# Seven products for the first 512 context rows of a Perceiver layer, one between any two heads, and a head's turn on VectorE one head later

## The chip, the core and the metric

The kernel runs on one core of a Trainium2 chip. The metric is the device time of one execution in microseconds (us), as a median over runs. TensorE multiplies, VectorE (DVE in the profile), ScalarE (ACT) and GpSimd (POOL) work on elements, and SyncE (SP) issues most transfers (DMA). Each engine works through its own queue in order and waits on semaphores for the others. TensorE writes to PSUM banks of 128 x 512 float32, which VectorE and ScalarE empty. All data are float32.

## The reference, cut to what matters

A layer of a Perceiver: 256 tokens of width 512 attend to themselves (causally) and to 4096 context rows; a state-space block and a mixture of experts follow. Only the attention's beginning is touched.

```python
xn = layernorm(x)                                    # 256 x 512
q  = rope(rms_norm((xn @ wq) by 16 heads of 128))
k  = rope(rms_norm((xn @ wk) by 4 heads)),  v = xn @ wv
k_ctx = rms_norm((ctx @ wk_ctx) by 4 heads)          # ctx: 4096 x 512
v_ctx = ctx @ wv_ctx
out = softmax([q k_ctx^T, q k^T + causal] / sqrt(128)) @ [v_ctx, v]
```

## The kernel before

The context is cut into eight chunks of 512 rows (`CK`). For chunk c, `kT` holds the keys turned, `v` the values and `r` the keys' factors. Attention runs in nine stages: stage 0 over the tokens' own keys, stage s over chunk s-1. While a stage's scores and values run on TensorE, the next chunk's keys and values are made between them.

Chunks 1 to 7 (`fast_steps`) use a scheme of seven products instead of eight: the chunk's rows and its inner dimension form a 2x2 block matrix (a11 to a22), and the weights form another, b11 and b21 being the two halves of wk_ctx and b12 and b22 those of wv_ctx. Keys are a11 b11 + a12 b21 and so on. Sums of the blocks, S1 to S4 on the left and T1 to T4 on the right, are multiplied, and the products are added up into keys and values. Each of the seven is split in seven again. T1, T2 and T4 come from `weight_sums` on POOL (L338 to L340) and T3 from one VectorE sum in place in `last_sum` (L389).

Chunk 0, made before stage 0, does not use the scheme. `context_pieces(0)` gives four key pieces, four value pieces and four transposes, one of each for every 128 rows; a piece is a projection of four matmuls 128x128 by 128x512 (`project`, L225), emptied by ScalarE (L319 for keys, L325 for values).

The tokens' projections come as "heads": `k_of(t)` and `q_of(j, t)` for two row tiles t and four groups j. A head (`self_block`) is one projection of four matmuls into a bank of `ps_mm` (two banks), then `norm_rope`: ScalarE copies the bank to `raw` (L536) and squares it (L262); VectorE does four rope steps (L541 to L544) and scales the square sums (L199); POOL takes the power -1/2 (L200) and multiplies (L545). Then the result is turned so that the head dimension is on partitions: for all but the last group by `turn_heads`, which is a VectorE block transpose (L268) and five DMAs on SP (L271, L273), else by TensorE transposes (`selfT`, L575).

The order is written out by hand in one tuple of steps, value and key pieces between the heads:

```python
for f in (ctx_v[0], lambda: k_of(0), lambda: k_of(1), last_key, *q[0], ctx_v[1], weights_of, lambda: self_value(0),
          q[1][0], one, q[1][1], one, lambda: self_value(1), weights_of, q[2][0], one, q[2][1], one, ctx_v[2],
          q[3][0], two, q[3][1], two, ctx_v[3]):
```

Ahead of the tuple stand the layernorm of both tiles, the key pieces 0 to 2, the transposes of xn into xT (`turn_xn`: L216 on TensorE, L220 on VectorE) and the rope tables (L528, L529). `one`, `two` and `weights_of` prepare the second level's weights on POOL and ScalarE. The framework's planner puts each engine's instructions in a queue largely in this order, moving one ahead where another must wait; `tc.issue_after(ins)` puts what is traced under it behind `ins` on the same engine. PSUM pools in this path: `ps_tp` one bank, `ps_mm` two, `ps_sc` three (scores), `ps_oT` two. A branch on the size of the norm weights picks this path (`bounded`); the other is not run here.

Loads are issued by SP in program order: pieces of ctx chunk 0 and of wk_ctx, x, the rest of ctx, wv_ctx, wk, wq0, wv, wq1 to wq3, and the context chunks 1 and 2.

Of the kernel before, what the change touches and what calls it, by code (L numbers as in the profile page):

```python
# [75 lines left out]
def perceiver_layer(ctx: ExitStack, tc: tile.TileContext, a: dict, out: bass.AP):  # L76
# [64 lines left out]
    def layer(ctx, bounded):  # L141
# [71 lines left out]
        def turn_xn(t, tp, halves=False):  # L213

            for k in range(KD):
                TE.transpose(tp[:, k * P:(k + 1) * P], xn[:, t, k * P:(k + 1) * P], ident)  # L216

            for copy, ks in (((V.tensor_copy, slice(0, KD // 2)), (S.copy, slice(KD // 2, KD))) if halves else
                             ((V.tensor_copy, slice(0, KD)),)):
                copy(xT[:, ks, t * P:(t + 1) * P], tp.rearrange("p (k n) -> p k n", k=KD)[:, ks])  # L220

        def project(ps, lhs, rhs_of):

            for k in range(KD):
                TE.matmul(ps, lhs(k), rhs_of(k), start=(k == 0), stop=(k == KD - 1))  # L225
# [14 lines left out]
        qT = qp.tile([P, NT, NH, P], FP, tag="qT", name="qT")  # L240
        aT = qT

        ctx_tiles = {0: ctx0}
# [12 lines left out]
        def head_squares(raw, apart=False):  # L256
# [53 lines left out]
        def context_pieces(c):  # L310

            ct = ctx_tiles.pop(c)
            v, r, raws, key_transpose, _ = context_tiles(c)

            def key_piece(i):
                ps = ps_mm.tile([P, 512], FP, tag="mm", name="ps_k")
                project(ps, lambda k: ct[:, i, k, :], lambda k: wkc[:, k, :])
                raws[i] = raw = krp.tile([P, NKV, HD], FP, tag="kraw" if i == 1 else "kn", name="kraw")
                S.copy(raw, ps.rearrange("p (h d) -> p h d", d=HD))  # L319
                key_rms(raw, r[:, i, :])  # L320

            def value_piece(i):
                ps = ps_mm.tile([P, 512], FP, tag="mm", name="ps_v")
                project(ps, lambda k: ct[:, i, k, :], lambda k: wvc[:, k, :])
                S.copy(v[:, i, :], ps)  # L325

            return [[lambda i=i, f=f: f(i) for i in range(CK // P)] for f in (key_piece, value_piece, key_transpose)]

        fast = {}

# [50 lines left out]

        each = lambda steps: [None for _ in steps]

        def last_sum():

            V.tensor_tensor(b12, b22, b12, ALU.subtract)  # L389
            each(second_sums("wv"))  # L390

        three = ring([(ps_mm, "mm"), (ps_mm, "mm"), (ps_tp, "tp")] if bounded else [(ps_mm, "mm")])

        def fast_steps(c, behind=None):
# [136 lines left out]
        heads_done = []  # L531

        def norm_rope(ps, t, tb):

            raw = krp.tile([P, REP, HD], FP, tag="kraw", name="raw")
            S.copy(raw, ps)  # L536
            r = small.tile([P, REP], FP, tag="r", name="r")
            power_half(r, head_squares(raw), 1.0 / HD, 1e-6, REP)
            cs, sn = (tb[:, i, t, :].unsqueeze(1).to_broadcast([P, REP, HD]) for i in range(2))
            o, u = take_ro(), take_ru()  # L540
            V.tensor_tensor(o, raw, cs, ALU.mult)  # L541
            V.tensor_tensor(u[:, :, 0:HALF], raw[:, :, HALF:HD], sn[:, :, 0:HALF], ALU.mult)
            V.tensor_tensor(u[:, :, HALF:HD], raw[:, :, 0:HALF], sn[:, :, HALF:HD], ALU.mult)
            V.tensor_tensor(o, o, u, ALU.add)  # L544
# [7 lines left out]
        ctx_k, ctx_v, ctx_t = context_pieces(0)  # L552
        for t in range(NT):
            normed = layernorm(t)
        for i in range(3):
            ctx_k[i]()
        for t in range(NT):
            turn_xn(t, ps_sc.tile([P, 512], FP, tag="sc", name="lnT"))
        rope_table(tab_k, kw_bc)
        rope_table(tab_q, qw_bc)  # L560
        with tc.issue_after(normed.ins):
            weight_sums(*sums)

        def self_block(t, w, tb, dst):
            ps = ps_mm.tile([P, 512], FP, tag="mm", name="ps_self")
            project(ps, lambda k: xT[:, k, t * P:(t + 1) * P], lambda k: w[:, k, :])
            o = norm_rope(ps.rearrange("p (h d) -> p h d", d=HD), t, tb)

            if bounded and w is not wq[3]:
                return turn_heads(dst, o, qd.pop())  # L570

            def turn():
                tp = ps_tp.tile([P, REP, P], FP, tag="tp", name="selfT")
                for h in range(REP):
                    TE.transpose(tp[:, h, :], o[:, h, :], ident)  # L575
                S.copy(dst, tp)
            return turn
# [10 lines left out]
        turns = ctx_t[0:3]  # L588

        def last_key():  # L590
            ctx_k[3]()
            return ctx_t[3]

        placed = fast_weights(sums)
        early = {"t": second_sums("t"), "t4": second_sums("t4")}
# [1 line left out]
        def behind_head(group, n=1):  # L597
            with tc.issue_after(heads_done[-1]):
                for _ in range(n):
                    next(early[group])  # L600

        weights_of = lambda: next(placed)
        one, two = lambda: behind_head("t"), lambda: behind_head("t4", 2)
        for f in (ctx_v[0], lambda: k_of(0), lambda: k_of(1), last_key, *q[0], ctx_v[1], weights_of, lambda: self_value(0),
                  q[1][0], one, q[1][1], one, lambda: self_value(1), weights_of, q[2][0], one, q[2][1], one, ctx_v[2],
                  q[3][0], two, q[3][1], two, ctx_v[3]):
            turn = f()
            if f not in (weights_of, one, two):
                turns.append(turn)
            while len(turns) > 2:  # L610
                turn = turns.pop(0)
                if turn:
                    turn()
# [17 lines left out]

        pin = tc.keep_in_program_order
        pin(nc.sync.dma_start(by_channel, a["by_channel"]))
        pin(nc.sync.dma_start(by_head, a["by_head"].partition_broadcast(P)))


        next(placed)
# [14 lines left out]
        def bounded_attention(beside):  # L652

            pp = pool("pp", 4)
            bq = small.tile([P, 3], FP, tag="bq", name="bq", bufs=1)
            V.tensor_reduce(bq[:, 0:1], qw_bc, AX.X, ALU.max, apply_absolute_value=True)
            V.tensor_reduce(bq[:, 1:2], kw_bc, AX.X, ALU.max, apply_absolute_value=True)
# [50 lines left out]
            for s in range(NC + 1):  # L708
# [39 lines left out]
        def general_attention():  # L748
            with ExitStack() as gctx:
# [11 lines left out]
                stats = {}  # L761
                for turn in turns:
                    turn()
                last_sum()
# [1050 lines left out]
```

## Time and profile before

| | |
|---|---|
| median of 3 runs | 960.36 us (959.47 to 961.25) |
| profiled execution | 961.0 us |
| its span on the core | 959.2 us |
| granted TensorE clock | 0.998 |
| TensorE busy | 939.9 us (98%) |
| VectorE, ScalarE, POOL busy | 571.4, 383.0, 429.3 us |
| data moved | 124.93 MB |

The span runs from the first to the last instruction that the profile holds; 1.8 us of the execution lie around it. In rows of the profile, "x8" counts records. A float32 matmul leaves two records, a float32 transpose one. "L225" is a line of the kernel, here that of the helper that records all projections, so tiles' names (ps_k, ps_v, ps_self) tell them apart. The arrow in square brackets names what ended an idle time.

| stretch, us | TensorE busy | VectorE | ScalarE | POOL |
|---|---|---|---|---|
| 0 to 5.4 | 0.00 | 0.70 | 0.00 | 1.33 |
| 5.4 to 18 | 12.55 | 6.06 | 5.66 | 2.27 |
| 18 to 24 | 6.00 | 3.80 | 3.17 | 5.84 |
| 24 to 30 | 6.00 | 2.13 | 3.09 | 4.17 |
| 30 to 40 | 10.00 | 5.51 | 8.42 | 4.58 |
| 40 to 50 | 10.00 | 3.64 | 3.95 | 4.09 |
| 50 to 60 | 10.00 | 6.13 | 5.82 | 3.91 |
| 60 to 70 | 10.00 | 7.17 | 4.97 | 6.73 |
| 70 to 80 | 10.00 | 6.93 | 5.28 | 7.64 |
| 80 to 90 | 10.00 | 7.62 | 7.57 | 9.82 |
| 90 to 100 | 9.89 | 9.62 | 6.10 | 9.95 |

The heads and pieces take until about 79 us; stage 0 follows, and stage 1 begins at about 101 us.

### The profile page before, as it was taken

What the parts mean: (1) busy time and instruction counts of PE and PEld (TensorE: products, weight loads), DVE (VectorE), ACT (ScalarE), POOL (GpSimd) and SP (SyncE); (2) the same over time, 40 slices, a digit from 0 to 9 for tenths busy, and PEclk for the clock granted to TensorE, in tenths of its full rate; (3) what the DMA queues carried; (4) which work ended last, traced back from release to release, by engine and by line L of the source; (5) the groups of instructions that cost most, each with busy time, mean ns of one, the idle gap of its engine ahead of it and who ended that gap; (6) DMA issues with size and microseconds to landing.
All of it is one profiled execution on the core that took longest, in us unless ns stands there. A gap on an engine that the chain in (4) does not pass through costs nothing.

```text
span 959.2 us, 10117 instructions
## 1 busy us (share of the span) xinstructions
PE 939.9 (98%) x3025; PEld 508.0 (53%) x3025; DVE 571.4 (60%) x1205; ACT 383.0 (40%) x872; POOL 429.3 (45%) x487
## 2 busy tenths in 40 slices
PE   7999999999999999999999999999999999999996
PEld 3444555555555555555555555544465655555442
DVE  4458766566566656665756656658497666632223
ACT  3646444344344444343443444443253742122221
POOL 3559956345444644634724723300013234545542
PEclk9999999999999999999999999999999999999999
DMA  9732053053034015104205203360046453899983
GB/s 328 241 78 47 0 176 87 1 154 89 1 86 141 15 35 174 35 14 152 77 1 153 67 1 88 81 228 0 0 157 209 165 196 122 327 328 366 362 322 109
DMA packets 130803, 124.93 MB, mean 130 GB/s; under 512 B 80017, under 2 KB 99250, under 8 KB 125490
## 3 DMA queue, kind: packets, MB, share of 16 engines
q1 hardware_dynamic: 119216, 77.96, 26.9%
q0 software_dynamic: 7904, 40.90, 11.7%
q10 hardware_dynamic: 3618, 5.33, 1.5%
q8 instruction: 26, 0.43, 0.2%
q14 instruction: 39, 0.32, 0.1%
HBM read 88.76 MB, written 35.41 MB: 129 GB/s over the span
## 4 chain that ended last, share of the span: by engine, by line
PE 95%; issue 1%; POOL 1%; DVE 1%; DMA 1%; ACT 0%; SPq 0%; POOLq 0%; DVEq 0%
PE oT L693 24%; PE scT L668 24%; PE ps_kv L459 15%; PE ps_egu L225 5%; PE ps_self L225 4%; PE ps_v L225 2%; PE ps_o L892 2%; PE ps_xbc L225 2%; PE ps_k L225 2%; PE ps_ye L1616 2%; PE ps_out L1089 1%; PE ps_z L225 1%; PE ps_sgu L225 1%; PE ps_ye L1619 1%; PE xgTp L1495 1%
## 5 line engine op out<-in xcount | busy, mean ns | idle before, releaser
L684 DVE TENSOR_TENSOR lacc<-lacc,prT 128x512 f32<-128x512 f32 x256 | 200.6, 785 | 197.3 <-ACT prT L674 196.2
L674 ACT ACTIVATE prT<-scT,bq,rk 128x512 f32<-128x512 f32 x256 | 198.4, 775 | 280.4 <-PE scT L668 269.5
L668 PE MATMUL scT<-qT,kT 128*128 128x512 f32 x536 | 273.5, 592 | 0.0
L693 PE MATMUL oT<-prT,v 128*128 128x512 f32 x528 | 269.4, 592 | 0.1
L693 PEld LDWEIGHTS oT<-prT,v 128*128 128x128 f32 x528 | 100.1, 190 | 125.8 <-issue 117.9
L668 PEld LDWEIGHTS scT<-qT,kT 128*128 128x128 f32 x536 | 101.2, 190 | 41.0 <-issue 30.6
L459 PE MATMUL ps_kv<-fast,ctx 128*128 128x256 f32 x350 | 99.6, 379 | 0.0
L459 PEld LDWEIGHTS ps_kv<-fast,ctx 128*128 128x128 f32 x350 | 66.4, 190 | 48.3 <-issue 39.9
L410 POOL TENSOR_TENSOR ctx<-ctx 128x128 f32<-128x128 f32 x21 | 11.4, 542 | 98.7 <-PE ps_kv L459 98.7
L200 POOL TENSOR_TENSOR rk<-pv,mhalf 128x4 f32<-128x4 f32 x32 | 37.4, 1180 | 28.0 <-DVE pv L199 28.0
L262 ACT ACTIVATE xn<-kraw 128x128 f32<-128x128 f32 x112 | 33.5, 301 | 39.4 <-POOL kraw L434 22.1
L459 PE MATMUL ps_kv<-wkv,ctx 128*128 128x256 f32 x168 | 48.9, 379 | 0.0
L444 POOL TENSOR_TENSOR v<-fast,v 128x768 f32<-128x768 f32 x21 | 40.9, 1960 | 16.2 <-DVE fast L488 15.6
L459 PEld LDWEIGHTS ps_kv<-wkv,ctx 128*128 128x128 f32 x168 | 31.8, 190 | 28.4 <-issue 25.0
L699 DVE TENSOR_TENSOR oacc<-oT,oacc 128x512 f32<-128x512 f32 x64 | 43.6, 682 | 0.0
L1599 DVE TENSOR_TENSOR hid<-si,ps_egu 128x128 f32<-128x128 f32 x18 | 5.2, 287 | 47.5 <-ACT si L1597 47.5
L459 PE MATMUL ps_kv<-fast,fast 128*128 128x256 f32 x112 | 33.3, 379 | 0.0
L459 PEld LDWEIGHTS ps_kv<-fast,fast 128*128 128x128 f32 x112 | 21.3, 190 | 17.8 <-issue 12.0
L268 DVE STREAM_TRANSPOSE tr<-kraw 128x512 f32<-128x512 f32 x28 | 18.3, 690 | 19.6 <-POOL kraw L433 19.6
L892 PE MATMUL ps_o<-wo,qT 128*128 128x512 f32 x64 | 28.8, 592 | 0.0
L1290 POOL DMA_INDIRECT xg_sb<-xg,place x16 | 15.1, 947 | 29.1 <-PE xgTp L1495 26.7
L225 PE MATMUL ps_self<-wq,xT 128*128 128x512 f32 x64 | 28.1, 592 | 0.0
(439 smaller groups left out, 1412.8 us busy)
## 6 DMA issues: line engine op xcount, KB each, us to landing
xg<-xn SPq DMA_DIRECT2D x6, 2560.0 KB, 9.4
ctx<-in_ctxT_dram SPq DMA_DIRECT2D x7, 1024.0 KB, 5.0
kd<-tr SPq DMA_DIRECT2D x112, 64.0 KB, 2.2
kT<-kd SPq DMA_DIRECT2D x28, 256.0 KB, 3.0
ye<-y_sb ACTq DMA_DIRECT2D x19, 256.0 KB, 8.3
wq<-in_wq_dram SPq DMA_DIRECT2D x4, 1024.0 KB, 14.4
wo<-in_wo_dram SPq DMA_DIRECT2D x4, 1024.0 KB, 7.9
w_in<-in_W_inT_dram SPq DMA_DIRECT2D x4, 1024.0 KB, 8.7
```

The costliest lines, as they stand in the source:

```text
L200: return G.tensor_tensor(dst, v[:, :n], mhalf[:, :n], ALU.pow)
L225: TE.matmul(ps, lhs(k), rhs_of(k), start=(k == 0), stop=(k == KD - 1))
L262: S.activation(sq[:, h, :], raw[:, h, :], AF.Square, accum_out=ss[:, h:h + 1])
L444: G.tensor_tensor(to[:, 1:4], q, base[:, 1:4], ALU.add)
L459: TE.matmul(b[n], sets[name][i], y, start=start, stop=True, skip_group_check=True)
L668: scored.append(TE.matmul(sc, kT[:, g, i * P:(i + 1) * P], qT[:, t, heads4(g), :].rearrange("p h q -> p (h q)"), start=True, stop=True).ins)
L674: S.activation(pr, sc, AF.Exp, bias=shift, scale=SCALE if r is None else r[:, i, g:g + 1])
L684: V.tensor_tensor(la, la, pr, ALU.add)
L693: TE.matmul(outs[g, t], v[:, i, g * HD:(g + 1) * HD], pr, start=(n == 0), stop=last)
L699: V.tensor_tensor(ov, outs.pop((g, t)), ov, ALU.add)
L892: TE.matmul(m["ps_o", t], aT[:, t, h, :], wo[j][:, h % 4, :], start=(h == 0), stop=(h == NH - 1))
L1616: TE.matmul(ps[i], h[:, i, :], wd[i], start=True, stop=False)
```

## The change

Chunk 0 is made by the seven products as well, one level deep: each product is two row blocks (j = 0, 1) of two matmuls 512 wide. p1 and p2 run before xn is turned: p1(j) = a11 b11 is copied by ScalarE to v, then p2(j) = a12 b21 is added into the same bank, and the sum is copied as the first keys. The others stand one between any two heads. They are emptied by VectorE, which adds each to what v holds. The sums S1 to S4 are made by VectorE in a tile that borrows a buffer of the context chunks, T3's sum moves up behind the second head, and the remaining POOL sums of wv_ctx move into the first sums of chunk 1. The loads change their order: x ahead of the second half of wk_ctx, the second half of ctx chunk 0 and wk (in two halves) ahead of wv_ctx, chunk 2 behind the small tables of a later block. A head's turn by VectorE is kept back until the next head's operations have been issued, and several small VectorE operations are put behind the copies of xT. The keys' transposes write to `ps_sc` instead of `ps_tp`.

```diff
     load_ctx0(0, 1)
     load_wkc(0, 1)
     load_wkc(1, 1)
-    load_wkc(2, 2)
+    load_ctx0(1, 1)
     nc.sync.dma_start(x_sb, a["x"].rearrange("(t p) d -> p t d", p=P))
-    load_ctx0(1, 1)
-    load_ctx0(2, 2)
-    nc.sync.dma_start(wvc, a["wv_ctx"].rearrange("(k p) n -> p k n", p=P))
+    load_wkc(2, 1)
+    load_wkc(3, 1)
...
         def load_ctx(c):
             ct = ctxp.tile([P, CK // P, KD, P], FP, tag="ctx", name="ctx")
-            nc.sync.dma_start(ct, a["ctxT"][c])
+            with tc.issue_after(settled[0]) if c == 2 else nullcontext():
+                nc.sync.dma_start(ct, a["ctxT"][c])
...
-        wk = wpiece(a["wk"], "wk")
+        load_ctx0(2, 2)
+        wk = wpool.tile([P, KD, 512], FP, tag="w", name="wk")
+        for k in (0, 2):
+            nc.sync.dma_start(wk[:, k:k + 2, :], a["wk"][k * P:(k + 2) * P, :].rearrange("(k p) n -> p k n", p=P))
+        nc.sync.dma_start(wvc, a["wv_ctx"].rearrange("(k p) n -> p k n", p=P))
...
+        first_sums = ctxp.tile([P, CK // P, KD, P], FP, tag="ctx", name="first_sums")
...
-                tp = ps_tp.tile([P, NKV, P], FP, tag="tp", name="kTp")
+                tp = (ps_sc if bounded else ps_tp).tile([P, NKV, P], FP, tag="sc" if bounded else "tp", name="kTp")
...
+        def first_step(sums):
...
+            def bank(held=False):
+                p, tag = (ps_mm, "mm") if held or not bounded else (ps_sc, "sc")
+                return p.tile([P, 512], FP, tag=tag, name="ps_first")
+
+            def product(ps, lhs, rhs, j, start=True):
+                for k in range(2):
+                    TE.matmul(ps, lhs[:, j, k, :], rhs[:, k, :], start=(start and k == 0), stop=(k == 1),
+                              skip_group_check=True)
+                return ps
...
+            def p1(j):
+                x[j] = product(bank(True), a11, b11, j)
+                S.copy(v[:, j, :], x[j])
+            def p2(j):
+                product(x[j], a12, b21, j, False)
+                S.copy(flat(key(j)), x.pop(j))
+            def p6(j):
+                V.tensor_tensor(v[:, j, :], product(bank(), S2, T2, j), v[:, j, :], ALU.add)
+            def p7(j):
+                V.tensor_tensor(v[:, 2 + j, :], product(bank(), S3, b12, j), v[:, j, :], ALU.add)
+            def p4(j):
+                V.tensor_tensor(flat(key(2 + j)), product(bank(), a22, T4, j), v[:, 2 + j, :], ALU.add)
+                return key_done(2 + j)
+            def p5(j):
+                z[j] = product(bank(), S1, T1, j)
+                V.tensor_tensor(v[:, 2 + j, :], z[j], v[:, 2 + j, :], ALU.add)
+            def p3(j):
+                product(z[j], S4, b22, j, False)
+                V.tensor_tensor(v[:, j, :], z.pop(j), v[:, j, :], ALU.add)
+            def sums12():
+                V.tensor_tensor(S1, a21, a22, ALU.add)
+                V.tensor_tensor(S2, S1, a11, ALU.subtract)
+            def sums34():
+                V.tensor_tensor(S3, a11, a21, ALU.subtract)
+                return V.tensor_tensor(S4, a12, S2, ALU.subtract)
+            def t3():
+                V.tensor_tensor(b12, b22, b12, ALU.subtract)
...
                 left("P6", S2)
+                if c == 1:
+                    each(second_sums("wv"))
...
-            V.tensor_tensor(o, raw, cs, ALU.mult)
+            with tc.issue_after(summed.ins):
+                V.tensor_tensor(o, raw, cs, ALU.mult)
...
-        for i in range(3):
-            ctx_k[i]()
+        for f in (p1, p2) if bounded else ():
+            for j in range(2):
+                f(j)
...
         for t in range(NT):
-            turn_xn(t, ps_sc.tile([P, 512], FP, tag="sc", name="lnT"))
-        rope_table(tab_k, kw_bc)
-        rope_table(tab_q, qw_bc)
+            turned = turn_xn(t, ps_sc.tile([P, 512], FP, tag="sc", name="lnT"))
+        with tc.issue_after(turned.ins):
+            key_turns = [key_done(j) for j in range(2)] if bounded else []
+            rope_table(tab_k, kw_bc)
+            rope_table(tab_q, qw_bc)
+            sums12()
+            summed = sums34()
...
             if bounded and w is not wq[3]:
-                return turn_heads(dst, o, qd.pop())
+                by_blocks.append(lambda: turn_heads(dst, o, qd.pop()))
+                return
...
+        def last_first():
+            with tc.issue_after(roped[-1]):
+                t3()
...
-        for f in (ctx_v[0], lambda: k_of(0), lambda: k_of(1), last_key, *q[0], ctx_v[1], weights_of, lambda: self_value(0),
-                  q[1][0], one, q[1][1], one, lambda: self_value(1), weights_of, q[2][0], one, q[2][1], one, ctx_v[2],
-                  q[3][0], two, q[3][1], two, ctx_v[3]):
+        for f in (of_heads[0], *key_turns[0:1], of_heads[1], *key_turns[1:2], last_first,
+                  q[0][0], lambda: p6(0), q[0][1], lambda: p6(1), weights_of, lambda: self_value(0),
+                  q[1][0], one, lambda: p7(0), q[1][1], one, lambda: p7(1), lambda: self_value(1), weights_of,
+                  q[2][0], one, lambda: p4(0), q[2][1], one, lambda: p4(1),
+                  q[3][0], two, lambda: p5(0), q[3][1], two, lambda: p5(1), *both(p3)):
             turn = f()
-            if f not in (weights_of, one, two):
+            while len(by_blocks) > (1 if f is not q[3][1] else 0):
+                by_blocks.pop(0)()
...
-                    if s == 0 and n == 8:
-                        with tc.issue_after(masked[-1]):
-                            last_sum()
```

More of the change, by code (lines that the diff above doesn't have):

```diff
@@ L219, in turn_xn @@
                              ((V.tensor_copy, slice(0, KD)),)):
-                copy(xT[:, ks, t * P:(t + 1) * P], tp.rearrange("p (k n) -> p k n", k=KD)[:, ks])
+                turned = copy(xT[:, ks, t * P:(t + 1) * P], tp.rearrange("p (k n) -> p k n", k=KD)[:, ks])
+            return turned
         def project(ps, lhs, rhs_of):
@@ L241, in layer @@
         aT = qT
-        ctx_tiles = {0: ctx0}
+        ctx_tiles, settled = {0: ctx0}, []
         def load_ctx(c):
             ct = ctxp.tile([P, CK // P, KD, P], FP, tag="ctx", name="ctx")
-            nc.sync.dma_start(ct, a["ctxT"][c])
+            with tc.issue_after(settled[0]) if c == 2 else nullcontext():
+                nc.sync.dma_start(ct, a["ctxT"][c])
             ctx_tiles[c] = ct
-        wk = wpiece(a["wk"], "wk")
+        load_ctx0(2, 2)
[3 more added lines that the diff above has]
+        nc.sync.dma_start(wvc, a["wv_ctx"].rearrange("(k p) n -> p k n", p=P))
         wq = [wpiece(a["wq"][:, 0:512], "wq0")]
@@ L308, in context_tiles @@
             return v, r, raws, key_transpose, key_blocks
[L310 to L327, printed above, removed]
         fast = {}
@@ L385, in layer, with key, key_done @@
         each = lambda steps: [None for _ in steps]
-        def last_sum():
-            V.tensor_tensor(b12, b22, b12, ALU.subtract)
-            each(second_sums("wv"))
+        def first_step(sums):
+            ct = ctx_tiles.pop(0)
+            v, r, raws, key_transpose, key_blocks = context_tiles(0)
+            T1, T2, T4 = sums
+            S1, S2, S3, S4 = carve(first_sums, *[OP] * 4)
+            a11, a12, a21, a22 = (ct[:, i:i + 2, k:k + 2, :] for i in (0, 2) for k in (0, 2))
+            x, z = {}, {}
+            def bank(held=False):
[6 more added lines that the diff above has]
+                return ps
+            def key(i):
+                raws[i] = krp.tile([P, NKV, HD], FP, tag="kn", name="kraw")
+                return raws[i]
+            def key_done(i):
+                key_rms(raws[i], r[:, i, :])
+                return lambda: key_transpose(i)
+            flat = lambda raw: raw.rearrange("p h d -> p (h d)")
+            def p1(j):
[25 more added lines that the diff above has]
+                V.tensor_tensor(b12, b22, b12, ALU.subtract)
+            return p1, p2, p3, p4, p5, p6, p7, sums12, sums34, t3, key_done
@@ L392, in layer @@
+        each = lambda steps: [None for _ in steps]
         three = ring([(ps_mm, "mm"), (ps_mm, "mm"), (ps_tp, "tp")] if bounded else [(ps_mm, "mm")])
@@ L529, in rope_table @@
                 V.scalar_tensor_tensor(tb[:, 1, :, half(i)], rope[:, :, 1, :], 2.0 * i - 1.0, wb[1 - i], ALU.mult, ALU.mult)
-        heads_done = []
+        heads_done, roped = [], []
         def norm_rope(ps, t, tb):
@@ L540, in norm_rope @@
             o, u = take_ro(), take_ru()
-            V.tensor_tensor(o, raw, cs, ALU.mult)
+            with tc.issue_after(summed.ins):
+                V.tensor_tensor(o, raw, cs, ALU.mult)
             V.tensor_tensor(u[:, :, 0:HALF], raw[:, :, HALF:HD], sn[:, :, 0:HALF], ALU.mult)
             V.tensor_tensor(u[:, :, HALF:HD], raw[:, :, 0:HALF], sn[:, :, HALF:HD], ALU.mult)
-            V.tensor_tensor(o, o, u, ALU.add)
+            roped.append(V.tensor_tensor(o, o, u, ALU.add).ins)
             heads_done.append(G.tensor_tensor(o, o, r.unsqueeze(2).to_broadcast([P, REP, HD]), ALU.mult).ins)
@@ L551, in layer @@
         kv[0] = (kT0, v0, None)
-        ctx_k, ctx_v, ctx_t = context_pieces(0)
+        p1, p2, p3, p4, p5, p6, p7, sums12, sums34, t3, key_done = first_step(sums)
         for t in range(NT):
             normed = layernorm(t)
-        for i in range(3):
-            ctx_k[i]()
-        for t in range(NT):
-            turn_xn(t, ps_sc.tile([P, 512], FP, tag="sc", name="lnT"))
-        rope_table(tab_k, kw_bc)
-        rope_table(tab_q, qw_bc)
+        for f in (p1, p2) if bounded else ():
+            for j in range(2):
+                f(j)
+        for j in () if bounded else range(2):
+            p1(j)
+            p2(j)
+            key_done(j)()
+        for t in range(NT):
+            turned = turn_xn(t, ps_sc.tile([P, 512], FP, tag="sc", name="lnT"))
[5 more added lines that the diff above has]
+            summed = sums34()
         with tc.issue_after(normed.ins):
@@ L587, in layer @@
         q = [[lambda j=j, t=t: q_of(j, t) for t in range(NT)] for j in range(4)]
[L588 to L592, printed above, removed]
+        turns, by_blocks = [], []
         placed = fast_weights(sums)
@@ L600, in behind_head @@
                     next(early[group])
+        def last_first():
+            with tc.issue_after(roped[-1]):
+                t3()
         weights_of = lambda: next(placed)
         one, two = lambda: behind_head("t"), lambda: behind_head("t4", 2)
-        for f in (ctx_v[0], lambda: k_of(0), lambda: k_of(1), last_key, *q[0], ctx_v[1], weights_of, lambda: self_value(0),
-                  q[1][0], one, q[1][1], one, lambda: self_value(1), weights_of, q[2][0], one, q[2][1], one, ctx_v[2],
-                  q[3][0], two, q[3][1], two, ctx_v[3]):
+        both = lambda f: (lambda: f(0), lambda: f(1))
+        of_heads = [(lambda: k_of(0)), (lambda: k_of(1)), *q[0], *q[1], *q[2], *q[3]]
+        for f in (of_heads[0], *key_turns[0:1], of_heads[1], *key_turns[1:2], last_first,
[3 more added lines that the diff above has]
+                  q[3][0], two, lambda: p5(0), q[3][1], two, lambda: p5(1), *both(p3)):
             turn = f()
-            if f not in (weights_of, one, two):
+            while len(by_blocks) > (1 if f is not q[3][1] else 0):
+                by_blocks.pop(0)()
+            if f not in (weights_of, one, two, last_first):
                 turns.append(turn)
-            while len(turns) > 2:
+            while len(turns) > 3:
                 turn = turns.pop(0)
@@ L633, in layer @@
         pin(nc.sync.dma_start(by_channel, a["by_channel"]))
-        pin(nc.sync.dma_start(by_head, a["by_head"].partition_broadcast(P)))
+        settled.append(pin(nc.sync.dma_start(by_head, a["by_head"].partition_broadcast(P))).ins)
         next(placed)
@@ L655, in bounded_attention @@
             bq = small.tile([P, 3], FP, tag="bq", name="bq", bufs=1)
-            V.tensor_reduce(bq[:, 0:1], qw_bc, AX.X, ALU.max, apply_absolute_value=True)
-            V.tensor_reduce(bq[:, 1:2], kw_bc, AX.X, ALU.max, apply_absolute_value=True)
+            with tc.issue_after(turned.ins):
+                V.tensor_reduce(bq[:, 0:1], qw_bc, AX.X, ALU.max, apply_absolute_value=True)
+                V.tensor_reduce(bq[:, 1:2], kw_bc, AX.X, ALU.max, apply_absolute_value=True)
             shift = bq[:, 2:3]
@@ L763, in general_attention @@
                     turn()
-                last_sum()
                 for s in range(NC + 1):
```

## The prediction

> **What bounds the kernel now.** I read the page's first and fourth parts first, then the chain of waits in order of time for the first 130 us, the list of what TensorE waited for, and last single rows of ScalarE, VectorE and POOL. From the page, busy time and the chain that ended last:
> ```profile
> PE 939.9 (98%) x3025; PEld 508.0 (53%) x3025; DVE 571.4 (60%) x1205; ACT 383.0 (40%) x872; POOL 429.3 (45%) x487
> ...
> PE 95%; issue 1%; POOL 1%; DVE 1%; DMA 1%; ACT 0%; SPq 0%; POOLq 0%; DVEq 0%
> ```
> TensorE is busy 939.9 of 959.2 us and is 95% of the chain. The chain in order of time (start, length, what) shows the stage that the change rewrites:
> ```profile
> 1.26 4.06 DMA wkv<-in_wk_ctx_dram
> 5.31 0.14 issue
> 5.45 12.42 PE ps_k L225 x24
> 17.87 0.87 PE lnT L216 x8
> 18.74 3.44 PE ps_v L225 x8
> ...
> 68.77 6.87 PE ps_self L225 x16
> 75.64 3.43 PE ps_v L225 x8
> 79.07 0.44 PE selfT L575 x4
> ```
> From 5.45 us, when the first weight lands, to 79.07 us one TensorE piece follows the other. One float32 matmul 512 wide is two records, so the four of ps_v (x8) take 3.43 us, 0.86 each. The span 5.45 to 79.07 adds up: 32 context and 48 projection matmuls make 68.6 us, 24 transposes of xn and keys 2.8, and the first four records run at 0.85 us instead of 0.43, which with the slowed fifth is 2.1; 73.5 of 73.6 us. There is no slack to win here, only work to remove. And nothing waits behind it:
> ```profile
> PE ps_k L225 <- DMA wkv<-in_wk_ctx_dram: 5.4, 1, 5.4
> ...
> PE ps_dt L225 <- DVE xT L220: 0.5, 1, 0.5
> ```
> In this list of TensorE's waits the first row is the only one before 130 us; the others lie behind 700 us. So a microsecond saved or lost on TensorE in this stage moves everything behind it by one. The second row, from a later turn of x, is used below.
>
> **The change part by part.**
>
> *Products.* Eight projections of four matmuls (32) become seven products by two row blocks by two matmuls (28): 4 x 0.858 = 3.43 us less on TensorE. The 24 transposes of keys and xn and the 8 of q stay. The keys' transposes go to the three ps_sc banks instead of the one of ps_tp, for which one of them waited 0.7 before with other work in between: nothing. So the products are the whole gain; what follows takes from it, and each wait named has all of TensorE's queue behind it.
>
> *p1 to p2.* p2(j) adds into the bank that p1(j) filled, and ScalarE must copy the bank to v in between. ScalarE's first copies in the trace:
> ```profile
> 11.09 1.28 ACT L319 ACT_TABLE_LOAD   x1 [11.09 <-DMA tables<-in_tables_dram]
> 12.38 0.59 ACT L319 COPY kraw<-ps_k 128x512 f32<-128x512 f32 x1
> ```
> The table load stands in front of the first copy: 1.88 us from the bank's end to the copy's end. p1(0) is four records, the fourth starting at 8.14 and lasting 1.19 (the longest record of L225), so ScalarE can start at 9.4 and is done at 11.28; p1(1) keeps TensorE until 10.84; p2(0) starts at 11.35. A gap of 0.51 us. Was ScalarE held by the tables' transfer, as the row says? That was issued at 4.70 and took 6.9, so it landed at 11.6, after the load had begun; the eighth record, started at 10.44 and 0.59 long, ends at 11.03. I take TensorE as the releaser. Ends: 0 (no wait) and 2.2 us (ScalarE free only at 11.09 again, p2 at 13.04).
>
> *Turn of xn.* Before, v's first projection stood between the transposes of xn and k's projection, and hid the copy of xT. Now k follows at once. At 742 us the transposes started at 742.23, the copy at 742.87, the reader 0.06 after the copy's end (the wait of 0.5 above). The copy here is 128x512, 0.675 us at L220: from the start of the transposes 0.64 + 0.675 + 0.06 = 1.38 us, less 0.87 for both tiles' transposes: a gap of 0.50. If k waits for both tiles' copies it is 0.60 more (19.32 to 19.92 between the two). Nothing on VectorE is in front of the copies any more: before, they waited to 19.32 behind the square sums of the keys (L199); the change queues those, the rope tables, the four new sums and L656/L657 behind them.
>
> *Loads.* SP's order changes. MB queued up to and with each piece, and its landing (issue time plus time to landing, or its waiter's start): 0.52 at 5.4, 1.31 at 7.8, 1.84 at 9.2 (x), 2.62 at 11.5, 3.67 at 16.9 (wv_ctx), 4.72 at 19.5 (wk), 5.77 at 22.2 (wq0), 6.82 at 25.0 (wv). The new order gives x at 1.57 (about 8.5), the last of wk_ctx at 2.10 (about 9.9), the halves of wk at 3.15 and 3.67 (14.2 and 16.9), wv_ctx at 4.72 (19.5), wq0 as before. TensorE by the new order: p2 done at 14.78, k(0) from 16.15 to 19.58, a key's transposes 0.49, k(1) to 23.5, q0 at 24.0, p6(0) at 27.4. So x (its layernorm took 9.23 to 12.7), both halves of wk (wanted at 16.15 and 17.9) and wq0 (24.0) are hidden, the tightest by 1.0 us. wv_ctx, put behind wk, is wanted by POOL first; see the slower rival. The second context load leaves SP's jammed queue (24 us) and comes after stage 0; its tile is wanted a stage later, so no cost.
>
> *Sums on VectorE.* Four of 128x512, 0.69 each by L544: 2.8 us, from about 20 to 23, before k(0)'s rope. VectorE is busy 2.13 of 6 us there (24 to 30). Two raw buffers let ScalarE empty q0's bank at 28 only when k(0)'s rope (about 25) has read the first: 3 us of cover. POOL's three sums of weights run at the same time:
> ```profile
> 19.39 2.39 POOL L339 TENSOR_TENSOR oacc<-wkv,oacc 128x1024 f32<-128x1024 f32 x1
> ...
> 66.60 1.26 DVE L542 TENSOR_TENSOR lacc<-raw,oacc 128x256 f32<-128x256 f32 x1
> ...
> 76.90 0.42 DVE L542 TENSOR_TENSOR lacc<-raw,oacc 128x256 f32<-128x256 f32 x1
> ```
> One form takes 0.42 with no POOL read beside it and 1.26 with one, so each sum may take 0.8 more, 3.4 in all, about the cover. The Trainium skill, "SBUF — State Buffer", section "Who interferes with whom", is stricter and speaks against this placement: a VectorE instruction with two SBUF inputs stands still for the whole GpSimd instruction that reads SBUF. By it each sum could cost a full POOL sum, 2.4, so four 9.6 us, and k(0)'s rope would end near 33; the value projection that reuses q0's bank comes at about 34, so its sum would be the same as by the row.
>
> *Evictions.* Ten go to VectorE, 0.68 each by the PSUM-reading sum L699 (64 of them, 43.6 us), in place of four copies of ScalarE: 6.8 us, and 1.48 for the moved L389, in the stretch from 18 to 80 us, in which VectorE is busy 35.3 of 62. Their banks rotate among three, one every 5 us: hidden, but for one. p3(1) adds into the bank that p5(1) filled and VectorE must have read. With T the end of the last q projection: p5(1) to T+1.72, q's transposes 0.44, p3(0) to T+3.9. VectorE gets the raw block at T+0.9, its four rope steps last to T+3.3, then the square sums' 0.16, a turn of 0.71, and the eviction 0.68: T+4.1 to T+4.8. A gap of 0.2 to 0.9; I take 0.40, because a ready score can go in. Ends: 0, and 2.6 if the rope runs as at 76.29 to 79.6 (slowed by POOL) and everything stands ahead of the eviction. The scores that follow need the same three banks, but VectorE is then free of L389 (1.48), which before stood among the masks; I count nothing for either.
>
> *Turns behind the next head.* Before, VectorE waited 8.9 us in four turns for POOL (L268 on L545). Now the next rope goes first. The turn's five DMAs leave one head later; the last turn is then near 78, no later than the 81.80 of before, and its readers come after 90. Off TensorE's path: nothing. POOL's moved sums of wv_ctx stand where they ran before (102.91, behind P6): nothing.
>
> Sum: -3.43 + 0.51 + 0.50 + 0.40 = -2.02 us. The profiled execution took 961.0, 0.64 above the median of the three runs, 960.36; so its span of 959.2 should become 957.2, and the median 958.3.
>
> **The rivals.** *All gaps closed.* The copy, xT and p5 arrive in time: -3.4, 957.0. Against it: 1.88 us of table load and copy cannot fit under p1(1)'s 1.7.
>
> *The gaps at their upper ends.* ScalarE is held to 11.09 (+1.7), or k waits for both copies (+0.6), or the last eviction is late (+2.2): with one of the dear ones 958.3 + 1.7 to 2.2 = 960.0 to 960.5, no difference. For it: the row that names the tables. Against it: their landing at 11.6.
>
> *Slower: T2 late.* p6(0) stands in TensorE's queue at 27.4 with everything behind it, and needs T2, POOL's second sum, 4.94 us after wv_ctx lands (16.92 to 21.86). At 19.5 it is ready at 24.4, with 3.0 us of cover. The transfers share the engines, and wv_ctx now has wk's place. If it lands at 24.6 (wv's place, 25.0, is there) the gain is gone; from 26.5 on the kernel is slower by over 0.2%; at the landing of wq1 (11.42 + 16.3 = 27.7) TensorE waits 5.2 and the time is 958.3 + 5.2 = 963.5. For it: 1 MB pieces took 13.8 to 16.3 from issue. Against it: landings followed the queue's order in every row.
>
> **How the numbers follow.** About 0.2% (1.9 us) is what a measurement can tell from no change: the border is 958.4, and the forecast lies just on the faster side. Forecast 0.40 (its own range 957.4 to 959.0, of which 0.10 falls within 0.2%), gaps closed 0.22, gaps at their upper ends 0.20, T2 late 0.18. Faster: 0.30 + 0.22 = 0.52; within: 0.10 + 0.20 = 0.30; slower 0.18. The range: 956.7, all gaps closed less the 0.3 by which runs differ, to 961.4, a little above the dear gaps; outside it is most of the slower case.
>
> **What would show it.** Right: 28 context matmuls; a TensorE wait near 11 us on ScalarE's copy of about 0.5, one of about 0.5 on xT near 16; p6(0) near 27 without a wait; first score near 77. Wrong: p2 starting at 13; p6 waiting for POOL; a wait of 2 us or more in front of p3(1) or the first scores; or new TensorE waits behind 100 us, which I hold to be none.

## The result and the profile after

The changed kernel takes 967.72 us (median of four runs, 967.29 to 969.71), the kernel before beside it 960.17 (959.47 to 961.25): ratio 1.0082, 95% interval 1.0064 to 1.0099. It is slower by 7.5 us, where 2 us less was forecast. The profiled execution took 967.9 us, its span 966.2 against 959.2.

The page's first and fourth parts: busy time of each engine, and the chain that ended last by engine.

```profile
PE 939.0 (97%) x3017; PEld 507.8 (53%) x3017; DVE 578.6 (60%) x1219; ACT 379.9 (39%) x868; POOL 426.7 (44%) x487
...
PE 93%; DVE 2%; DMA 2%; POOL 1%; issue 1%; ACT 1%; SPq 0%; POOLq 0%; DVEq 0%; ACTq 0%
```

TensorE has eight records fewer, the four matmuls saved, but is busy for only 0.9 us less than before, and DVE and DMA now hold 2% of the chain each. Which wait is it? The list of what TensorE waited for (total, times, longest):

```profile
PE ps_first L385 <- DMA wkv<-in_wk_ctx_dram: 5.4, 1, 5.4
PE scT L735 <- DMA qT<-qd: 5.2, 1, 5.2
PE oT L760 <- DVE prT L744: 1.8, 1, 1.8
```

Before had only the first of these in this part of the run. The second is a score that waits for queries still on their way from memory, the third a value product that waits for a mask. The chain of waits around them, in order of time (start, length, what):

```profile
84.23 0.71 DVE tr L274
84.96 0.31 SPq L277
...
86.39 3.95 DMA qd<-tr
...
90.90 2.80 DMA qT<-qd
...
93.74 2.07 PE scT L735 x2
95.82 1.71 PE oT L760 x2
97.53 1.14 PE scT L735 x2
...
99.46 4.36 DVE prT L744
...
103.87 1.13 PE oT L760 x2
```

The turn of the last head of group 2 starts on VectorE at 84.23; its DMAs out and back end at 93.70. The eighth score of stage 0 reads these queries, and TensorE, free since 88.56, stands in front of it for 5.18 us. In before the same turn started at 81.80, and SyncE's queue shows its DMAs earlier. Of before, then of after (start, length of issuing):

```profile
82.53 1.93 SPq L271 DMA_DIRECT2D qd<-tr  x4
86.40 0.38 SPq L273 DMA_DIRECT2D qT<-qd  x1
```

```profile
84.96 1.94 SPq L277 DMA_DIRECT2D qd<-tr  x4
90.90 0.38 SPq L279 DMA_DIRECT2D qT<-qd  x1
```

Three rows of before that the reading rests on: VectorE's turn, the way back of its queries (the last number is the time from issue to landing), and the score that reads them.

```profile
81.80 0.70 DVE L268 STREAM_TRANSPOSE tr<-lacc 128x512 f32<-128x512 f32 x1
```

```profile
qT<-qd SPq DMA_DIRECT2D x1, 256.0 KB, 2.7
```

```profile
90.20 1.02 PE L668 MATMUL scT<-qT,kT 128*128 128x512 f32 x2
```

Before, the queries landed at 89.1 (86.40 + 2.7) and their score came at 90.20: 1.1 us of slack. After, three things eat it. The turn is 2.43 later (84.23 - 81.80), the way from turn to landing is 9.47 instead of 7.3, so 2.17 longer, and the score comes up at 88.56 instead of 90.20, 1.64 earlier. 2.43 + 2.17 + 1.64 - 1.1 = 5.1, against a measured wait of 5.18.

The wait then costs more than itself. Windows of TensorE (stretch, sum, busy and records, granted clock, DMA share, GB/s):

```profile
84.00:88.00 4.00, 4.00 (x11) 1.00 0.46 73
88.00:92.00 4.00, 0.56 (x2) 0.89 0.03 8
92.00:96.00 4.00, 2.26 (x3) 0.50 0.46 115
96.00:100.00 4.00, 4.00 (x8) 0.76 0.54 225
100.00:104.00 4.00, 2.21 (x6) 1.00 0.00 0
```

The clock granted is 1.00 before the wait, 0.50 after it, and 1.00 again from 100 us. The three pieces from 93.74 take 4.74 us to the start of the next (98.48) instead of three times 0.86: 2.2 us lost. (The Trainium skill, "TensorE: Matmul & The Clock Gate", "Part 1: The HAM clock gate", states half clock after an idle window of about 3.4 us and full clock after a busy one as long; these rows agree, but in e6 below a wait of 2.89 us was enough.)

The balance up to the first pieces of stage 1 starts at the first scores. TensorE's rows of before, then of after:

```profile
79.34 2.74 PE L668 MATMUL scT<-qT,kT 128*128 128x512 f32 x6
```

```profile
77.88 2.74 PE L735 MATMUL scT<-qT,kT 128*128 128x512 f32 x6
```

The first score starts 1.46 earlier, and a second group of `selfT` transposes (0.44) that in before stood between the scores at 82.89 is done by then: 1.9 us won. Lost are 5.2, 2.2 and 1.8. -1.9 + 5.2 + 2.2 + 1.8 = +7.3. The first product of stage 1 (`ps_kv`) starts at 108.35 instead of 101.14, 7.2 later, and the whole span is 7.0 longer.

### The profile page after: what moved, and what is told of

The parts are those of the page before. It is cut to its first block, busy times and chain, and to the rows that moved or that the text cites. A ratio compares the mean times of both kernels' runs of the same rounds, so it can differ in the third digit from the quotient of the medians.

```text
span 966.2 us, 10121 instructions
## 1 busy us (share of the span) xinstructions
PE 939.0 (97%) x3017; PEld 507.8 (53%) x3017; DVE 578.6 (60%) x1219; ACT 379.9 (39%) x868; POOL 426.7 (44%) x487
## 4 chain that ended last, share of the span: by engine, by line
PE 93%; DVE 2%; DMA 2%; POOL 1%; issue 1%; ACT 1%; SPq 0%; DVEq 0%; ACTq 0%; POOLq 0%
PE scT L735 23%; PE oT L760 23%; PE ps_kv L508 15%; PE ps_egu L225 5%; PE ps_self L225 4%; PE ps_o L954 2%; PE ps_first L385 2%; PE ps_xbc L225 2%; PE ps_ye L1678 2%; PE ps_out L1151 1%; PE ps_z L225 1%; PE ps_egu L1577 1%; PE ps_sgu L225 1%; PE ps_ye L1681 1%; PE xgTp L1557 1%
## 5 line engine op out<-in xcount | busy, mean ns | idle before, releaser
L751 DVE TENSOR_TENSOR lacc<-lacc,prT 128x512 f32<-128x512 f32 x256 | 198.1, 775 | 200.0 <-ACT prT L741 198.7
L455 POOL TENSOR_TENSOR ctx<-fast 128x128 f32<-128x128 f32 x28 | 19.4, 694 | 19.7 <-PE ps_kv L508 19.3
```

The source lines that it names most:

```text
L455: G.tensor_tensor(s1, x[:, 1, 0], x[:, 1, 1], ALU.add)
L751: V.tensor_tensor(la, la, pr, ALU.add)
```

## The experiments

Theory A: what was won at the products is there, and the loss is one late transfer, the last turn's queries; the low clock and the long mask follow from TensorE's wait. Rival D: keeping each turn back behind the next head made it late. Theory E came with the first results: behind the wait removed stands another, of VectorE beside POOL in stage 1. Theory F is its counterpart: POOL has no room earlier. Other letters are explained where the expectations use them. Runs of e1 to e4 share one chip, e5 to e7 another, e8 to e10 a third, on which the kernel before took 965.50 instead of about 960; ratios are to the kernel before on the same chip.

**e1: a third place for turned heads.** A turned head lies in a buffer `tr`, of which there are two, until its DMAs have landed. Here every third one goes to a part of `xn` that is free by then.

```diff
...
-            tr = krp.tile([P, REP * HD], FP, tag="tr", name="tr")
+            third[0] += own
+            tr = (xn[:, 1, :] if own and third[0] % 3 == 0 else
+                  krp.tile([P, REP * HD], FP, tag="tr", name="tr"))
...
```

> The changed kernel, with a third place for a head's block transpose: every third of the eight turned heads goes into the rows xn[:, 1, :], which nothing reads at that time, instead of one of the two tr buffers. Theory A (the last turn comes too late because VectorE's queue holds it back for one of two tr buffers, and the score that needs its queries waits for its DMAs): the turn of q2's second tile moves from 84.2 to about 78 us, its queries land near 87 us, TensorE's wait of 5.2 us goes, and with it the half clock after it and the mask of 4.4 us; 8 to 9 us less than the changed kernel's 967.7, so 958 to 959. Rival B (the extra work of VectorE in stage 0 makes masks and turns late, whatever the buffers): the waits move to other masks and turns, 964 to 968. Rival C (the five DMAs of the turn themselves became slow, 9.5 us from turn to landing instead of 7.3): the wait shrinks only by the 6 us that the turn moves, and the time is 960 to 963.

959.08 us against 959.93, ratio 0.9991 (0.9982 to 1.0001). SyncE's queue and the list of TensorE's waits of e1:

```profile
78.32 1.94 SPq L281 DMA_DIRECT2D qd<-tr  x4
82.31 0.38 SPq L283 DMA_DIRECT2D qT<-qd  x1
```

```profile
PE ps_kv L512 <- DVE fast L521: 1.2, 1, 1.2
PE ps_first L389 <- DVE v L423: 0.3, 1, 0.3
PE selfT L639 <- POOL lacc L599: 0.3, 1, 0.3
```

Only the place of a turned head was edited. The last turn's DMAs leave at 78.32 instead of 84.96 (other turns moved forward too: the fifth one's DMAs leave at 51.73 instead of 62.26), and the wait for queries, the low clock and the wait for the mask are all gone. Rival B, an overloaded VectorE, would have kept most of the loss, and rival C, slow DMAs, 1 to 4 us of it; neither fits 959.08. So the ring of two buffers kept the turn's place in VectorE's queue back; that the planner reckons with the time until a buffer's DMAs have landed is my reading of its order, not shown. But the first row is new: a wait of 1.24 us at 103.44, in stage 1. VectorE's rows of e1 in front of it:

```profile
98.63 1.59 DVE L753 TENSOR_TENSOR lacc<-prT 128x512 f32<-128x512 f32 x1
100.14 3.46 DVE L755 TENSOR_TENSOR lacc<-lacc,prT 128x512 f32<-128x512 f32 x2
103.53 0.68 DVE L768 COPY oacc<-oT 128x512 f32<-128x512 f32 x1
104.13 0.41 DVE L521 TENSOR_TENSOR fast<-ps_kv,fast 128x256 f32<-128x256 f32 x1
```

Two sums that take 0.68 each when POOL is quiet (e6 has one at 103.60) take 3.46 together, while POOL works without a pause from 97.5 to 106. That is theory E. It leaves 1.9 - 1.2 = 0.7 us of the gain; 0.9 was measured, with an interval that just includes no difference.

**e2: the heads of group 2 turned by TensorE.** No late transfer can arise, since the last two groups' turns need no DMA; TensorE pays for eight transposes more.

```diff
-            if bounded and w is not wq[3]:
+            if bounded and w is not wq[3] and w is not wq[2]:
```

> The changed kernel, with the third query group (q2) turned like the fourth, by TensorE transposes and not by VectorE and DMAs. Theory A: no score waits for a DMA any more; 8 transposes more on TensorE (0.11 each, 0.9 us) and about 958 to 960. Rival B: VectorE's load falls only by two turns of 0.7 us, so most of the loss stays, 964 to 967.

958.56 us, ratio 0.9988 (0.9978 to 0.9998). The waits for queries and mask are gone, the wait of 1.3 us in stage 1 is there. A second way around the same transfer, with the same end.

**e3: each turn at once.**

```diff
-            while len(by_blocks) > (1 if f is not q[3][1] else 0):
+            while by_blocks:
```

> The changed kernel, with the keeping back of a head's turn undone: the turn is issued right after its own head's operations, as before the change. Theory A: the two tr buffers, not the order of the text, set when the last turn is issued, so it stays behind the same mask on VectorE; 965 to 968. Rival D (the turn is late because the change keeps it back by a head, some 5 us): the wait at the eighth score goes, 958 to 961.

968.24 us, ratio 1.0074 (1.0049 to 1.0099). TensorE's waits of e3:

```profile
PE scT L735 <- DMA qT<-qd: 5.1, 1, 5.1
PE ps_first L385 <- DMA wkv<-in_wk_ctx_dram: 4.8, 1, 4.8
PE oT L760 <- DVE prT L744: 1.9, 1, 1.9
```

The same two waits with the keeping-back undone. Rival D falls: the line that keeps a turn back does not decide when the last one runs (on VectorE at 84.5 here).

**e4: the third place in the kernel before.** The same edit as e1.

> The kernel before, with the third place for the block transpose. There the last turn's queries land 1.1 us ahead of the score that needs them. Theory A: the turn moves ahead, but nothing waited for it, so no difference, 959.5 to 961. A gain of over 2 us would mean that the turns cost the kernel before something too, which its trace does not show.

960.16 us, ratio 1.0001 (0.9992 to 1.0011). The last turn's DMAs leave at 75.61 instead of 82.53, and nothing is won: before had 1.1 us of slack there, so e1's place is worth something in the changed kernel alone.

**e5: the scores that read the last turn go last.** Neither the turn nor its buffers are touched, only the order of the twelve scores of stage 0.

```diff
+                    if s == 0:
+                        steps = steps[0:7] + steps[9:12] + steps[7:9]
```

> The changed kernel, with one edit in the order of stage 0's scores: the two of the third head group and second row tile, which read the queries of the last turn, go from the eighth and ninth place to the last two. VectorE's turn keeps its place in the queue. Theory A (one score waits for the last turn's DMAs, and TensorE's queue stands behind it): the score is wanted 3 x 1.72 = 5.2 us later, near 93.7 us, just when its queries land; wait, half clock and long mask go, 958 to 960. Rival B (VectorE is overloaded in stage 0): 964 to 968.

959.69 us against 960.67, ratio 0.9987 (0.9978 to 0.9996). Here the turn stays late on VectorE, at 83.7. SyncE's queue and TensorE's wait of e5:

```profile
84.47 1.94 SPq L277 DMA_DIRECT2D qd<-tr  x4
88.50 0.38 SPq L279 DMA_DIRECT2D qT<-qd  x1
```

```profile
PE ps_kv L508 <- DVE fast L517: 1.2, 1, 1.2
```

This is the sharpest of the five. The queries land at 91.3 (88.50 + 2.8), 3.4 us after the eighth place in TensorE's queue came up (87.92) and 1.8 ahead of their reader in its new place (93.07), and the 8 us are gone. The turn is as late as in after; its DMAs took some 2 us less, so 2 of the 5 us that the reader was put off were not needed. Theory A holds. What remains is E's wait, now in three kernels.

**e6 and e7: POOL's second-level sums of wk_ctx earlier.** In stage 1 the four sums of `second_sums("wk")`, 1.3 to 1.75 us each on POOL, are part of what VectorE runs beside. Here all four go behind the two heads of group 2; e6 on top of e1, e7 on top of e2.

```diff
-                  q[2][0], one, lambda: p4(0), q[2][1], one, lambda: p4(1),
+                  q[2][0], one, wk2, lambda: p4(0), q[2][1], one, wk2, lambda: p4(1),
...
-        with tc.issue_after(heads_done[-1]):
-            each(second_sums("wk"))
```

> As e1_third_buffer, and POOL's four sums for the second level of wk_ctx (6 us) run behind the two heads of q2 instead of behind the last head, so that POOL's unbroken stretch of sums (from 77 us on) ends some 6 us earlier. In e1 TensorE waited 1.24 us at 103.4 for a VectorE sum queued behind a pair of sums that took 3.46 us beside POOL. Theory E (those sums stand still while POOL runs without a pause): the wait goes, 1.2 us less than e1, so 957.5 to 958.2. Rival F (VectorE is late at the start of stage 1 for its own work): no change, 959.

> As e2_last_group_by_tensore, with the same move of POOL's four sums. Theory E: e2's wait of 1.26 us at 103.5 goes, 957.2 to 957.8. Rival F: no change, 958.6.

e6: 961.63 us, ratio 1.0012 (1.0003 to 1.0021). e7: 960.83, 1.0004 (0.9995 to 1.0013). Both missed. The wait in stage 1 is gone in both, which fits E; but TensorE's timeline of e6 shows the price (start, busy, and in brackets the idle time before and what ended it):

```profile
76.46 0.66 PE L639 MATMUL selfT<-ident,lacc 128*128 128x128 f32 x4 [2.89 <-POOL lacc L599]
...
81.66 2.74 PE L737 MATMUL scT<-qT,kT 128*128 128x512 f32 x6
```

POOL multiplies the last heads late, TensorE waits 2.89 us for it, and the first score comes at 81.66 instead of e1's 77.73. The wait is not all of it: the granted clock is 0.50 from 78 to 81 us, and the six records of `ps_first` behind the wait take 4.2 us to the start of the next piece (76.95 to 81.16) instead of six times 0.43, 1.6 more. So a wait of 2.89 us was long enough to cost the clock as well. I had counted POOL's room from 60 to 78 us by its share of busy time, and not by when it was free.

**e8, e9 and e10: two of the four sums earlier.** One behind each head of group 2, the other two stay; on top of e5, e2 and e1.

```diff
-                  q[2][0], one, lambda: p4(0), q[2][1], one, lambda: p4(1),
+                  q[2][0], one, wk1, lambda: p4(0), q[2][1], one, wk1, lambda: p4(1),
...
-            each(second_sums("wk"))
+            each(early["wk"])
```

> The kernel of e5 (scores that read the last turn go last), and two of POOL's four second-level sums of wk_ctx, 1.27 to 1.74 us each, go behind the two heads of q2, the other two stay behind the last head. Theory E (TensorE's 1.22 us wait at 104 us comes from VectorE standing beside POOL's sums): POOL is done 3.0 us earlier there, the wait falls to 0 to 0.3, and the time is 958.5 (e5's 959.69 less 0.9 to 1.2), ratio near 0.9976. Theory F (POOL has no room before the last head, as e6 showed with four sums): half of the 6 us still makes the last heads' multiplies late by 0 to 1.5 us, selfT waits as much, and the time stays at 959.7 or above, ratio 0.9987 or more.

> The kernel of e2 (the heads of q2 turned by TensorE too), and two of POOL's four sums of wk_ctx behind the heads of q2. Theory E: the 1.3 us wait at 103.5 us goes, 957.5, ratio near 0.9977. Theory F: the four turns of TensorE each want POOL's multiply, so half of e7's added waits of 2.1 us comes back, about 1.0: 958.5 or above, ratio 0.9988 or more.

> The kernel of e1 (a third place for turned heads), and two of POOL's four sums of wk_ctx behind the heads of q2. With all four moved (e6) selfT waited 2.9 us and the first score came at 81.66 instead of 77.73. Theory E: the stage-1 wait of 1.2 us goes, 957.9 to 958.2, ratio near 0.998. Theory F: selfT waits 1 to 1.5 us, the first score is at 78.7 to 79.2, and the time is 959 to 959.6, ratio 0.999 or more.

| kernel | median, us | before beside it | ratio | 95% interval |
|---|---|---|---|---|
| e8 | 964.94 | 965.50 | 0.9991 | 0.9981 to 1.0001 |
| e9 | 963.34 | 965.50 | 0.9978 | 0.9966 to 0.9991 |
| e10 | 963.72 | 965.50 | 0.9978 | 0.9965 to 0.9991 |

TensorE's waits of e10 between 60 and 112 us:

```profile
PE ps_first L389 <- DVE v L423: 0.5, 1, 0.5
PE oT L764 <- DVE lacc L748: 0.4, 1, 0.4
PE selfT L639 <- POOL lacc L599: 0.3, 1, 0.3
```

The wait in stage 1 is gone in all three; VectorE's pair of sums, 3.46 us in e1, takes 1.80 in e8, 2.62 in e9 and 2.61 in e10. `selfT` waits no longer than in e1 (0.3) in e8 and e10, and 1.4 in e9. In place of the wait stands a mask's of 0.4 to 0.5. Between 70 and 110 us TensorE is idle 1.20 us in e10 and 1.85 in e1. E and F are both right in part. e9 and e10 beat the kernel before by about 0.2%, some 2 us; the intervals of e1 and e10 overlap, so that the two sums alone bring something is likely and not shown. For e9 not even that can be said: from 60 to 112 us TensorE is idle 1.88 us in it as in e2, the lost wait replaced by `selfT`'s, and the two intervals overlap. e8 stayed near e5's ratio, and its trace shows why: other waits took the place of the 1.22 us, 0.48 for a mask, 0.38 for VectorE's copy of `oT` (L764) and 0.19 more in front of p3. TensorE is idle for 1.66 us between 70 and 110 in e8 and for 1.82 in e5.

## Why the prediction was wrong

**The products and the three gaps: right in sum, in part by chance.** Forecast -3.43 + 0.51 + 0.50 + 0.40 = -2.02; measured -1.9, the 1.46 at the first score and the 0.44 of `selfT` behind it. Each of the three gaps came out smaller, and what was not foreseen made up for it. TensorE's and ScalarE's timelines of after, at the start:

```profile
5.40 5.54 PE L385 MATMUL ps_first<-wkv,ctx 128*128 128x512 f32 x8 [5.40 <-DMA wkv<-in_wk_ctx_dram]
11.18 3.70 PE L385 MATMUL ps_first<-wkv,ctx 128*128 128x512 f32 x8 [0.23 <-ACT v L401]
14.71 1.04 PE L215 MATMUL lnT<-ident,xn 128*128 128x128 f32 x8
15.59 0.60 PE L305 MATMUL kTp<-ident,kraw 128*128 128x128 f32 x4
16.10 7.13 PE L225 MATMUL ps_self<-wk,xT 128*128 128x512 f32 x16
```

```profile
9.24 1.28 ACT L401 ACT_TABLE_LOAD   x1 [9.24 <-DMA tables<-in_tables_dram]
10.54 1.07 ACT L401 COPY v<-ps_first 128x512 f32<-128x512 f32 x2
```

p1 to p2: 0.23 instead of 0.51. ScalarE starts its load at 9.24, close to the 9.4 worked out, though the row again names the tables: TensorE's bank released it, as argued. The turn of xn: no gap instead of 0.50, since the planner put the first key's four transposes (15.59) into it. p5 to p3: a wait of 0.30 for VectorE's L419, 0.40 taken. Unforeseen was a wait of 0.30 of `selfT` for POOL's multiply. With it the waits come to 0.83, which would leave -2.6; the other 0.7 lies in pieces that take a little longer next to a wait (1.98 us for the four records behind p3's wait, 1.72 where one piece follows the other) and is not split up further.

**T2, the loads, the sums: right.** wv_ctx reached POOL at 17.95, earlier than the 19.5 taken, and p6 ran at 30.37 without a wait, three us later than worked out since both query heads went first. The four sums on VectorE took 0.68 to 0.76, not the 1.5 of the bound. Here luck helped: they ran from 26.85 to 29.5 and not from 20 to 23, and POOL's three sums of weights, beside which they were placed, had ended at 26.9, so the bound was not put to the test. One row behind it was misread too: the VectorE step at 76.90 that took 0.42 was not free of POOL, whose multiply started 0.08 us into it; one at 73.97, with POOL idle, took 0.41, so the size stands.

**The step that failed: "Turns behind the next head".** It said: "The turn's five DMAs leave one head later; the last turn is then near 78, no later than the 81.80 of before, and its readers come after 90. Off TensorE's path: nothing." Three errors stand in it. The last turn ran at 84.23: I placed it by when its data are ready, and not by VectorE's queue, where it stands behind the two evictions of p3, the turn before it and three masks, and where the ring of two `tr` buffers decides (e1, with a third place, brings it to 77.6). "Readers come after 90" was the time of before; what I had won myself on TensorE brought the reader to 88.5. And the slack in before was never worked out: the transfer landed at 89.1 for a score at 90.20, so 1.1 us was all there was, less than the gain forecast. A row of the issue queue and a row of TensorE, both in the trace of before, would have shown it. This one term, put at nothing, is 5.2 us, with 2.2 of clock and 1.8 of mask behind it. With it fails the premise that a microsecond saved in this stage "moves everything behind it by one": that held for the first seven scores, and the eighth stood still for its queries.

**"New TensorE waits behind 100 us, which I hold to be none": wrong.** In after it is the mask's 1.79 at 103.87, and in e1, e2 and e5, with the transfer out of the way, 1.2 to 1.3 in stage 1. The rows of after, VectorE and then POOL:

```profile
99.46 4.35 DVE L744 TENSOR_TENSOR prT<-prT,upper 128x512 f32<-128x512 f32 x1 [1.21 <-ACT prT L741]
103.74 0.68 DVE L764 COPY oacc<-oT 128x512 f32<-128x512 f32 x1
```

```profile
99.10 1.29 POOL L366 TENSOR_TENSOR fast<-wkv,fast 128x512 f32<-128x512 f32 x1
...
101.57 1.28 POOL L471 TENSOR_TENSOR fast<-ctx,fast 128x512 f32<-128x512 f32 x1
102.79 0.47 POOL L458 TENSOR_TENSOR ctx<-fast,ctx 128x128 f32<-128x128 f32 x1
```

I had weighed the rule of "Who interferes with whom" at the four sums, beside which POOL then ran nothing but powers four elements wide, and not here, where it ran sums.

**The rivals.** All gaps closed, gaps at their upper ends and T2 late all sit in the first 80 us; the case that came lies behind them. The slower rival chose a load in front of the stage, where the slack was 3.0 us, and not the transfer at its end, where it was 1.1.

## What to carry to other kernels

A piece that is made earlier wants its inputs earlier: for each transfer that lands just behind the stage, set landing against reader in the trace of before, and take any slack smaller than the gain as a new wait. A step that leaves a queue later, or keeps its place, is to be timed by the instructions in front of it and by the ring of buffers that it writes to, not by when its data are ready. A wait on TensorE is to be priced with the clock lost behind it, here 2.2 us more behind 5.2, and in e6 1.6 more behind 2.9; the waits of 1.8 us and less cost none.

## What the runs showed of the hardware that was not expected

A sum of two SBUF operands on VectorE, 0.68 us when POOL is quiet, stood 4.35 us while POOL ran six sums in a row (99.10 to 103.26), and ended 0.5 us after the last of them. (The Trainium skill, "SBUF — State Buffer", "Who interferes with whom", lets such an instruction wait for one GpSimd instruction; here the time runs over six.) At 83 to 89 us the same form took 0.94 to 0.96 with POOL just as busy, so how long it stands is not settled.

The fourth DMA of the last turn took 3.95 us to land in after and 3.94 in e3, where it took some 2.0 in before and e5. A load of instructions (one packet, 0.02 MB) moved on the same engines at about 88 us; but one moved between 78 and 92 us in before too. That it lengthened the way was not tried.
